# Layers 2 and 3 of a four-layer cross-attention kernel: two stages one after the other, or common slots ten tiles apart

## The chip, the cores and the metric

The kernel runs on one core of a Trainium2 chip, all in float32 but for one small mask. The metric is the device time of one launch in microseconds; the value of a kernel is the median of its runs. The core has five engines that run their own instruction lists in order and wait for one another by semaphores: PE (TensorE, matrix products and transposes by an identity, into PSUM), DVE (VectorE), ACT (ScalarE), POOL (GpSimd), and SP, which here only issues DMAs. PEld is PE's loading of weights.

## The reference

Four layers follow one another on `x` of shape (4, 1024, 256); the context has 77 rows per batch, and there are 16 heads. Layer 0 is attention over itself and the context, with a feed-forward part; layer 1 is a linear and a windowed attention. The change is in layers 2 and 3, here with projections cut to a line each:

```python
def layer2(x, ctx, mask, weights):            # mask, weights: (4, 16, 1024, 77)
    q, k, v = heads(x @ Wq.T + bq), heads(ctx @ Wk.T + bk), heads(ctx @ Wv.T + bv)
    scores = einsum('bhqd,bhkd->bhqk', q, k) / sqrt(16) * weights
    p = softmax(where(mask, -inf, scores))
    x = x + unheads(p @ v) @ Wo.T + bo
    return layernorm(x) * gamma + beta
def layer3(x, ctx):
    normed = x * rsqrt(mean(x * x) + 1e-6) * norm_w
    q, k, v = heads(normed @ wq), heads(ctx @ wk), heads(ctx @ wv)   # 64 per head
    return x + unheads(softmax(q @ k.T) @ v) @ wo
```

## The kernel before, in words

The 4096 rows are 32 tiles of 128 rows, eight to a batch; the whole of x stays in SBUF. What depends on the context alone has been folded and kept in DRAM during layer 0: `kept_k` and `kept_v` for layer 2, `kept_g` (wq times the keys, "G") and `kept_u` (the values times wo, "U") for layer 3. A tile's scores of both layers are 16 x 77 = 1232 columns.

The order of instructions is the order of the Python code (`tc.manual_schedule()`, L100); each engine takes its own in that order. After layer 1 the pool `late` is opened and the stage that concerns us runs, through L1841, as a chain of *slots*.

**Layer 2's slot, `slot2` (L1457).** In slot i work stands for tiles i, i-1, i-3, i-4 and i-5. For tile i PE makes the scores (`ps`, in a pair of PSUM banks, pool `big`, two of them), DVE multiplies them by the side weights (L1485) and masks them (`copy_predicated`, L1490), and takes the maxima of each head (`nm`, L1510 and L1514). For tile i-1 ACT makes 16 Exps of 77 columns (L1473), DVE sums and inverts (`den`, L1526 and L1527), POOL divides (L1528). For tile i-3 PE turns the ten chunks of 128 columns (`turned`, L1369: `psT` in three tiles of the PSUM pool `sm`, copied by ACT to `pT`). For tile i-4 PE multiplies by the values (`pvT`, pool `sm`), and ACT copies the result (`oT`, L1507). For tile i-5 PE multiplies by Wo (`po2`, in the one bank of pool `pv`), DVE adds to x (L1520) and POOL adds the bias (L1521). The side weights and mask of a tile, 770 KB, are loaded by SP one tile ahead (`load_sides`, L1449).

**Layer 3's slot, `slot3` (L1574).** For tile i PE makes the scores from the normed features `xT3` and G in two halves, DVE takes the maxima of each half from PSUM and subtracts them (L1599, L1600), ACT makes one Exp of 1232 columns (L1608), DVE sums and POOL divides (L1613). For tile i-2 PE turns the chunks, four before the first half of the scores, four between the halves and two after, and then multiplies by U (`po3`), DVE adds to x (L1623) and SP stores the tile.

**Between the slots** stand jobs that are doled out over a batch's eight slots: `prep2` (the next batch's queries: 16 transposes with copies on DVE, and 16 matmul instructions), `norm2` (L1532: the layernorm of a whole batch, when layer 2 is done with it: statistics on DVE, `inv_std` on POOL with a `pow`, `away` = -mean/std on POOL, then for each tile an Identity on ACT (L1543) and two products on POOL), `stats3` and `features3` (the RMS norm and `xT3` of a batch: `xn` on DVE, transposes `ptx` in `sm`, evicted on DVE with the weight), `loads2` and `loads3` (V, G and U of a batch), and the rest of layer 1 (`combine1`). Layer 3's first slots run beside the last five of layer 2, which only drain it.

PSUM is shared by all of these: `sm` has three tiles, used in turn by psT, pvT, ptx, pp2 and others, so a new one waits for the reader of the third last.

Of the kernel before, what the change touches and what calls it, by code (L numbers as in the profile page):

```python
# [17 lines left out]
P = 128  # L18
# [9 lines left out]
SC = 0.25  # L28
# [3 lines left out]
def tile_xattn_seq(ctx: ExitStack, tc: tile.TileContext, d: dict, out: bass.AP):  # L32
# [252 lines left out]
    def inv_std(rs, mv, eps, rms):  # L285

        if rms:
            nc.gpsimd.tensor_tensor(rs, mv[:, :, 0], mv[:, :, 0], ALU.mult)
            nc.gpsimd.tensor_tensor(rs, rs, mv[:, :, 1], ALU.add)
            nc.gpsimd.tensor_scalar_add(rs, rs, eps)  # L290
        else:
            nc.gpsimd.tensor_scalar_add(rs, mv[:, :, 1], eps)
        nc.gpsimd.tensor_tensor(rs, rs, nhalf, ALU.pow)
# [1084 lines left out]
    def new_scores():  # L1378
        s = late.tile([P, P * NC], F32, name="s", tag="s", bufs=4)
        nc.gpsimd.memset(s[:, HK:], 0.0)  # L1380
        return s
# [11 lines left out]
    def load_folded(b):  # L1393

        U = late.tile([P, NC, D], F32, name="U3", tag="qu")
# [6 lines left out]
        return U  # L1402

    def loads2(b):

        V = late.tile([P, NC, D], F32, name="V2", tag="qu").rearrange("p c n -> p (c n)")
        V = V[:, 0 : (NC + 1) * P].rearrange("p (c n) -> p c n", n=P)
# [18 lines left out]

    def prep2(b):

        x = xs[b]
        xT = late.tile([P, 2, T], F32, name="xT2", tag="xT")  # L1430
        yield from to_features(xT, lambda i: x[:, i, :], None, None, None, None)
        qT = late.tile([P, 2, T], F32, name="qT2", tag="gs")
        for o in range(2):
            for q in range(2):
                pp = sm.tile([P, 512], F32, name="pp2", tag="sm")
                for c in range(2):
                    mm(
                        pp, l2["Wq"][:, c, P * o : P * o + P], xT[:, c, 512 * q : 512 * q + 512],
                        start=(c == 0), stop=(c == 1),
                    )  # L1440
# [4 lines left out]
                if o and q:  # L1445
                    shared["b2", b] = qT
                yield

    def load_sides(i):  # L1449
        b, t = divmod(i, NT)  # L1450
        side = late.tile([P, HK + HK // 4], F32, name="side", tag="side")
# [5 lines left out]
    def slot2(i, tiles, at, gap2):  # L1457


        p1, p3, p4, p5 = (tiles.get(i - k) for k in (1, 3, 4, 5))  # L1460
        a = None
        if i < NB * NT:
            b, t = divmod(i, NT)
            a = tiles[i] = dict(b=b, t=t)
            qT, kb = shared["b2", b], shared["k2"]
            fs, mk = shared.pop(("side", i))
            if i + 1 < NB * NT:
                load_sides(i + 1)
            s = a["s"] = new_scores()
        if p1:  # L1470
            for h in range(H):
                hs = p1["s"][:, S * h : S * h + S]
                nc.scalar.activation(hs, hs, AF.Exp, bias=p1["nm"][:, h : h + 1], scale=SC)  # L1473
        if a:
            for o in range(2):
                ps = pair_tile()
                for e in range(2):
                    r = half_rows(e)
                    mm(
                        ps[:, e, 0 : 4 * S].rearrange("p (h s) -> p h s", s=S),  # L1480
                        qT[r, o, P * t : P * t + P],
                        kb[r, o, :, b, :],
                    )
                so = slice(o * HH * S, (o + 1) * HH * S)
                nc.vector.tensor_tensor(  # L1485
                    s[:, so].rearrange("p (i n) -> p i n", i=2), ps[:, :, 0 : 4 * S],
                    fs[:, so].rearrange("p (i n) -> p i n", i=2), ALU.mult,
                )
            sv = s[:, 0:HK]
            nc.vector.copy_predicated(sv, mk, low.to_broadcast([P, HK]))  # L1490
        gap2(at + 0.4)
        if p5:
            xt = xs[p5["b"]][:, p5["t"], :]
            po = pvp.tile([P, D], F32, name="po2", tag="pv")
            for o in range(2):
                mm(po, p5["oT"][:, o, :], l2["Wo"][:, o, :], start=(o == 0), stop=(o == 1))
            del tiles[i - 5]
        if p4:

            V = shared["v2", p4["b"]]  # L1500
            pv = sm.tile([P, 2, P], F32, name="pvT", tag="sm")
            for k in range(NC + 1):
                o, c = (0, k) if k < 5 else (1, k - 1)
                r = slice(0, rows_in(c))
                mm(pv[:, o, :], V[r, k, :], p4["pT"][r, c, :], start=k in (0, 5), stop=k in (4, NC))
            oT = p4["oT"] = late.tile([P, 2, P], F32, name="oT", tag="oT")
            nc.scalar.copy(oT, pv)  # L1507
        if a:
            nm = a["nm"] = small.tile([P, H], F32, name="nm", tag="m16")
            nc.vector.tensor_reduce(  # L1510
                nm, sv.rearrange("p (h k) -> p h k", k=S), axis=AX.X, op=ALU.max
            )

            nc.vector.tensor_scalar(nm, nm, 0.1 * NEG, -SC, ALU.max, ALU.mult)  # L1514
        if p3:
            pT = p3["pT"] = late.tile([P, NC, P], F32, name="pT", tag="pT", bufs=3)
            for g in range(3):
                turned(p3["s"], g, pT)
        if p5:
            nc.vector.tensor_tensor(xt, po, xt, ALU.add)  # L1520
            nc.gpsimd.tensor_tensor(xt, xt, rows["bo"], ALU.add)  # L1521
        gap2(at + 1.0)
        if p1:
            s3 = p1["s"][:, 0:HK].rearrange("p (h k) -> p h k", k=S)
            den = small.tile([P, H], F32, name="den", tag="den")
            nc.vector.tensor_reduce(den, s3, axis=AX.X, op=ALU.add)  # L1526
            nc.vector.reciprocal(den, den)  # L1527
            nc.gpsimd.tensor_tensor(  # L1528
                s3, s3, den.unsqueeze(2).to_broadcast([P, H, S]), ALU.mult
            )  # L1530

    def norm2(b):  # L1532

        x = xs[b]
        res = []
        yield from stats_job(res, lambda t: x[:, t, :], 1e-5, False)
        mv, rs = res
        away = small.tile([P, NT], F32, name="away", tag="away")
        nc.gpsimd.tensor_tensor(away, mv[:, :, 0], rs, ALU.mult)
        nc.gpsimd.tensor_scalar(away, away, -1.0, None, ALU.mult)  # L1540
        for t in range(NT):
            xt = x[:, t, :]
            nc.scalar.activation(  # L1543
                xt, xt, AF.Identity, bias=away[:, t : t + 1], scale=rs[:, t : t + 1]
# [3 lines left out]
            yield  # L1548


    def stats3(b):

        res = shared["st3", b] = []
        yield from stats_job(res, lambda t: xs[b][:, t, :], 1e-6, True)

    def features3(b):

        xT = shared["xT3", b] = late.tile([P, 2, T], F32, name="xT3", tag="xT")
        rs = shared["st3", b][1]
        yield from to_features(  # L1560
            xT, lambda t: xs[b][:, t, :], None, rs, cols["L3_xattn_norm_w"], None
        )

    def loads3(b):

        G = late.tile([P, 2, 8, 2, S], F32, name="G3", tag="gs")
        nc.sync.dma_start(
# [6 lines left out]
    def slot3(i, tiles, at, gap2):  # L1574
# [10 lines left out]
        for o in range(2):  # L1585
            if p2:
                turned(p2["s"], o, pT)
# [284 lines left out]
```

## Time and profile before

| | us |
|---|---|
| median of 3 runs | 2313.92 |
| lowest, highest | 2309.47, 2317.93 |
| the profiled execution's own time | 2315.16 |
| its span in the profile | 2313.4 |
| from layer 2's first scores to the end of the span (1723.3 to 2313.4) | 590.1 |

The page gives each engine's busy time, and groups instructions by line, engine, operation and tiles: count, busy time, mean duration, then the idle time of the engine just before them and who released it. In a window's row each engine's busy time is followed by its number of instructions. In a timeline row the first number is the start in us, the second the time until the end of the last of the merged instructions. A float32 matmul stands in the records as two instructions, so the ten products with U are x20. The granted clock was 0.981 over the whole span.

### The profile page before, as it was taken

The numbers are of one execution on the slowest core, as the hardware profiler recorded it, in microseconds if no ns is written. First come the engines' busy times: TensorE is split into PE (matmuls) and PEld (weight loads), VectorE is DVE, ScalarE is ACT, GpSimd is POOL, SyncE is SP. The second block draws the span as 40 slices with busy tenths as digits, with TensorE's granted clock in tenths as the row PEclk, the third lists the DMA queues.
The fourth block names the chain that finished last, engine by engine and source line by source line (L and its number), as shares of the span: only waits on it lengthen the run. The fifth ranks groups of instructions, "written<-read, shape, count | busy, mean of one in ns | idle before, by whom it ended". The sixth has DMA issues, their size and how long they took to land.

```text
span 2313.4 us, 41275 instructions
## 1 busy us (share of the span) xinstructions
PE 2167.0 (94%) x16874; PEld 1357.5 (59%) x16874; DVE 1511.2 (65%) x2492; ACT 1028.1 (44%) x1700; POOL 642.4 (28%) x927
## 2 busy tenths in 40 slices
PE   4999999999999999999989999999999998999999
PEld 2544444555555455554556675656556776788887
DVE  3756567755566555754376666777759999677664
ACT  1144444434444444344533444545548876432222
POOL 2011113111131112310152232333423655542221
PEclk9899999999999999999989999999999999999999
DMA  7221121100000000101000011101023334102200
GB/s 216 55 57 68 32 64 41 40 6 15 7 15 2 10 11 6 38 1 19 6 15 6 15 28 19 21 15 21 15 78 124 114 109 126 47 15 58 58 14 17
DMA packets 87858, 93.98 MB, mean 41 GB/s; under 512 B 35714, under 2 KB 77558, under 8 KB 87542
## 3 DMA queue, kind: packets, MB, share of 16 engines
q1 hardware_dynamic: 87670, 91.35, 15.1%
q8 instruction: 133, 2.18, 0.4%
q14 instruction: 55, 0.45, 0.1%
HBM read 55.31 MB, written 18.39 MB: 32 GB/s over the span
## 4 chain that ended last, share of the span: by engine, by line
PE 70%; DVE 14%; ACT 5%; issue 1%; POOL 1%; DVEq 0%; ACTq 0%
PE ps L51 27%; PE po L51 13%; PE pv L51 6%; PE pp L51 6%; PE ph L51 4%; DVE mpart L672 3%; PE psT L1375 2%; DVE ms L1138 2%; PE ppv L51 2%; PE pvT L51 2%; PE pvw L51 1%; DVE mrow L1142 1%; PE ptx L339 1%; PE pm L590 1%; PE pt L607 1%
## 5 line engine op out<-in xcount | busy, mean ns | idle before, releaser
L51 PE MATMUL ps<-qk 32*128 32x192 f32 (+9 forms) x6528 | 581.9, 428 | 57.8 <-DVE mpart L672 25.0
L738 ACT ACTIVATE pe<-ps 128x1024 f32<-128x1024 f32 (+2 forms) x384 | 363.3, 952 | 589.5 <-PE ps L51 581.5
L51 PEld LDWEIGHTS ps<-qk 32*128 32x128 f32 (+1 forms) x6528 | 315.9, 185 | 295.8 <-issue 75.5
L672 DVE TENSOR_REDUCE mpart<-ps 128x2 f32<-128x1024 f32 (+4 forms) x384 | 330.9, 884 | 241.9 <-PE ps L51 241.2
L741 POOL TENSOR_SCALAR_AFFINE_SELECT pe<-pe 128x256 f32<-128x256 f32 (+1 forms) x192 | 94.9, 495 | 665.5 <-ACT pe L738 664.6
L1214 ACT ACTIVATE pew<-ps 128x768 f32<-128x768 f32 x128 | 103.4, 812 | 196.4 <-PE ps L51 196.3
L1219 POOL TENSOR_SCALAR_AFFINE_SELECT pew<-pew 128x512 f32<-128x512 f32 x128 | 81.7, 638 | 338.0 <-ACT pew L1214 337.9
L1376 ACT COPY pT<-psT 128x512 f32<-128x512 f32 (+1 forms) x192 | 92.3, 518 | 175.4 <-PE psT L1375 174.9
L1138 DVE TENSOR_TENSOR ms<-ps,maskw 128x768 f32<-128x768 f32 x128 | 122.1, 954 | 69.7 <-PE ps L51 68.2
L51 PE MATMUL pv<-pe,va 128*32 128x512 f32 (+3 forms) x1536 | 157.1, 496 | 0.0
L51 PE MATMUL ph<-yT,w 128*128 128x256 f32 x512 | 143.1, 401 | 2.4 <-DVE va L401 1.0
L51 PE MATMUL po<-U,pT 128*128 128x256 f32 (+1 forms) x640 | 143.7, 379 | 0.2
L51 PE MATMUL ps<-G,xT 128*128 128x308 f32 x512 | 143.0, 423 | 0.0
L51 PEld LDWEIGHTS po<-w,hT 128*128 128x128 f32 x800 | 111.6, 192 | 47.7 <-issue 38.9
L1473 ACT ACTIVATE s<-s,nm 128x77 f32<-128x77 f32 x512 | 131.2, 347 | 17.3 <-DVE nm L1514 17.2
L51 PE MATMUL po<-w,hT 128*128 128x128 f32 (+1 forms) x800 | 138.0, 317 | 0.9 <-ACT hT L904 0.9
L665 DVE TENSOR_REDUCE mpart<-ps 128x8 f32<-128x1024 f32 x64 | 78.2, 1225 | 82.6 <-PE ps L51 82.4
L1613 POOL TENSOR_TENSOR s<-s,den 128x1232 f32<-128x1232 f32 x32 | 71.9, 2248 | 203.4 <-DVE den L1612 176.9
L51 PEld LDWEIGHTS po<-U,pT 128*128 128x128 f32 (+1 forms) x640 | 119.2, 190 | 15.5 <-ACT pT L1376 0.6
L51 PEld LDWEIGHTS ph<-yT,w 128*128 128x128 f32 x512 | 88.7, 192 | 63.9 <-issue 50.8
L1142 DVE TENSOR_REDUCE mrow<-ms 128x4 f32<-128x768 f32 x128 | 122.2, 955 | 4.4
L1375 PE MATMUL psT<-ident,s 128*128 128x128 f32 x640 | 92.9, 274 | 16.8 <-ACT oT L1507 13.0
(200 smaller groups left out, 3381.9 us busy)
## 6 DMA issues: line engine op xcount, KB each, us to landing
side<-in_fside_t SPq DMA_DIRECT2D x32, 616.0 KB
qk<-st SPq DMA_DIRECT2D x256, 64.0 KB
side<-in_mask_t SPq DMA_DIRECT2D x32, 154.0 KB
G<-kept_g SPq DMA_DIRECT2D x4, 1232.0 KB
U<-kept_u SPq DMA_DIRECT2D x4, 1152.0 KB
x<-in_x SPq DMA_DIRECT2D x8, 512.0 KB
out<-x SPq DMA_DIRECT2D x32, 128.0 KB
kept_g<-st SPq DMA_DIRECT2D x22, 154.0 KB
```

The costliest lines, as they stand in the source:

```text
L51: nc.tensor.matmul(o, lhsT, rhs, start=start, stop=stop, **kw)
L665: nc.vector.tensor_reduce(mpart[self.own][:, :, 2 * p : 2 * p + 2, 0].rearrange("p t j -> p j t"), ps.rearrange("p j (t n) -> p j t n", n= ...
L672: nc.vector.tensor_reduce(mpart[bl][:, i, 2 * p : 2 * p + 2, ci], ps[:, :, o : o + w], axis=AX.X, op=ALU.max,)
L738: nc.scalar.activation(pp[:n, :, o:512], ps[:n, :, o:512], AF.Exp, scale=SC)
L741: nc.gpsimd.affine_select(out=own, in_=own, compare_op=ALU.is_ge, fill=0.0, base=0, pattern=[[0, 2], [0, k], [1, P]], channel_multiplier=-1,)
L1138: nc.vector.tensor_tensor(v, ps.rearrange("p j (i n) -> p j i n", i=2)[:, :, :, 0:n], (maskw[:, 1:2] if w else maskw).unsqueeze(1).to_broa ...
L1142: nc.vector.tensor_reduce(mo, v, axis=AX.X, op=ALU.max, negate=True)
L1214: nc.scalar.activation(pp[:, :, :, 0 : P + WIN], ps.rearrange("p j (i n) -> p j i n", i=2)[:, :, :, 0 : P + WIN], AF.Exp, scale=SC,)
L1219: nc.gpsimd.affine_select(out=pf[:, :, 0:P], in_=pf[:, :, 0:P], compare_op=ALU.is_ge, fill=0.0, base=0, pattern=[[0, 4], [1, P]], channel_ ...
L1375: nc.tensor.transpose(ps[:, k, :], s[:, P * c : P * c + P], ident)
L1376: nc.scalar.copy(pT[:, 4 * group : 4 * group + n, :], ps[:, 0:n, :])
L1473: nc.scalar.activation(hs, hs, AF.Exp, bias=p1["nm"][:, h : h + 1], scale=SC)
```

## The change

One loop of 44 slots (`slot23`) takes the place of both chains: slot i has layer 2's tiles i (scores), i-1 (Exps, division), i-2 (transposes and values) and i-3 (Wo), and layer 3's tiles j = i-10 (scores), j-1 (division) and j-2 (transposes, product with U, store). The 16 Exps are issued in four fours. The norm after layer 2 and the RMS norm before layer 3 become one generator, `between(g)`, for four tiles at a time; it starts in slot 7+4g, and `more()`, which stands at three places of a slot, takes two steps of it, and one step of `prep2` and of `combine1`, each time. `prep2` works in two halves, and its transposes are copied by ACT. Tiles have tags of their own: s2 (3 buffers) and s3 (2), pT2 and pT3 (1 each), V2, G3 and U3 (2 each); the queries and xT3 lie in places that weights of layers 0 and 1 have left. V of the next batch and G and U of this one are loaded in slot 4 of each batch. PSUM pools are as before.

```diff
-    def new_scores():
-        s = late.tile([P, P * NC], F32, name="s", tag="s", bufs=4)
+    def new_scores(tag, bufs):
+        s = late.tile([P, P * NC], F32, name=tag, tag=tag, bufs=bufs)
...
-    def load_folded(b):
-        U = late.tile([P, NC, D], F32, name="U3", tag="qu")
+    def loads3(b):
+        G = late.tile([P, 2, 8, 2, S], F32, name="G3", tag="G3", bufs=2)
+        nc.sync.dma_start(
+            out=G.rearrange("p c f e s -> p (c f e) s"),
+            in_=kept_g.rearrange("p c f e (b s) -> p (c f e) b s", s=S)[:, :, b, :],
+        )
+        U = late.tile([P, NC, D], F32, name="U3", tag="U3", bufs=2)
...
-        return U
+        shared["b3", b] = (G.rearrange("p c f e s -> p c (f e s)"), U)
+        yield
     def loads2(b):
-        V = late.tile([P, NC, D], F32, name="V2", tag="qu").rearrange("p c n -> p (c n)")
-        V = V[:, 0 : (NC + 1) * P].rearrange("p (c n) -> p c n", n=P)
+        V = late.tile([P, NC + 1, P], F32, name="V2", tag="V2", bufs=2)
...
+    def turned_x(dst, rows, g):
+        for c in range(2):
+            pt = sm.tile([P, 4, P], F32, name="ptx", tag="sm")
+            for i in range(4):
+                nc.tensor.transpose(pt[:, i, :], rows[i][:, c * P : (c + 1) * P], ident)
+            src = pt.rearrange("p i n -> p (i n)")
+            if g is None:
+                nc.scalar.copy(dst[:, c, :], src)
+            else:
+                nc.vector.tensor_scalar(dst[:, c, :], src, g[:, c : c + 1], None, ALU.mult)
+            yield
     def prep2(b):
-        xT = late.tile([P, 2, T], F32, name="xT2", tag="xT")
-        yield from to_features(xT, lambda i: x[:, i, :], None, None, None, None)
-        qT = late.tile([P, 2, T], F32, name="qT2", tag="gs")
-        for o in range(2):
-            for q in range(2):
+        qT = wpool.tile([P, 2, T], F32, name="qT2", tag=("s2", "s4")[b % 2])
+        shared["b2", b] = qT
+        for q in range(2):
+            xT = late.tile([P, 2, 512], F32, name="xT2", tag="xT2", bufs=1)
+            yield from turned_x(xT, [x[:, 4 * q + i, :] for i in range(4)], None)
+            for o in range(2):
                 pp = sm.tile([P, 512], F32, name="pp2", tag="sm")
...
-    def slot2(i, tiles, at, gap2):
...
+    def stats4(st, mv, rs, g, eps, rms):
+        b, t0 = divmod(4 * g, NT)
+        for k in range(4):
+            nc.vector.bn_stats(st[:, k], xs[b][:, t0 + k, :])
+            nc.vector.bn_aggr(mv[:, k], st[:, k])
+            if k == 3:
+                inv_std(rs, mv, eps, rms)
+            yield
+    def between(g):
+        b, t0 = divmod(4 * g, NT)
         x = xs[b]
-        res = []
-        yield from stats_job(res, lambda t: x[:, t, :], 1e-5, False)
-        mv, rs = res
-        away = small.tile([P, NT], F32, name="away", tag="away")
+        st = small.tile([P, 4, 6], F32, name="st4", tag="st6")
+        mv = small.tile([P, 4, 2], F32, name="mv4", tag="mv", bufs=3)
+        rs = small.tile([P, 4], F32, name="rs4", tag="rs", bufs=3)
+        yield from stats4(st, mv, rs, g, 1e-5, False)
+        away = late.tile([P, 4], F32, name="away", tag="away")
         nc.gpsimd.tensor_tensor(away, mv[:, :, 0], rs, ALU.mult)
         nc.gpsimd.tensor_scalar(away, away, -1.0, None, ALU.mult)
-        for t in range(NT):
-            xt = x[:, t, :]
+        for k in range(4):
+            xt = x[:, t0 + k, :]
             nc.scalar.activation(
-                xt, xt, AF.Identity, bias=away[:, t : t + 1], scale=rs[:, t : t + 1]
+                xt, xt, AF.Identity, bias=away[:, k : k + 1], scale=rs[:, k : k + 1]
             )
             nc.gpsimd.tensor_tensor(xt, xt, rows["gamma"], ALU.mult)
             nc.gpsimd.tensor_tensor(xt, xt, rows["beta"], ALU.add)
             yield
-    def stats3(b):
...
-    def features3(b):
...
-    def slot3(i, tiles, at, gap2):
...
+        st = small.tile([P, 4, 6], F32, name="st4", tag="st6")
+        mv = small.tile([P, 4, 2], F32, name="mv4", tag="mv", bufs=3)
+        rs = small.tile([P, 4], F32, name="rs4", tag="rs", bufs=3)
+        yield from stats4(st, mv, rs, g, 1e-6, True)
+        xn = []
+        for k in range(4):
+            xt = small.tile([P, D], F32, name="xn", tag="xn", bufs=4)
+            normed(xt, x[:, t0 + k, :], None, rs, k)
+            xn.append(xt)
+            if k % 2:
+                yield
+        xT = shared["xT3"][:, g % 2]
+        yield from turned_x(xT, xn, cols["L3_xattn_norm_w"])
+    LAG = 10
...
+    def score2(a, i):
+        b, t = a["b"], a["t"]
+        qT, kb = shared["b2", b], shared["k2"]
+        fs, mk = shared.pop(("side", i))
+        if i + 1 < NB * NT:
+            load_sides(i + 1)
+        s = a["s"] = new_scores("s2", 3)
...
+    def exps2(a, heads):
+        for h in heads:
+            hs = a["s"][:, S * h : S * h + S]
+            nc.scalar.activation(hs, hs, AF.Exp, bias=a["nm"][:, h : h + 1], scale=SC)
+    def divided(a, tag):
+        s3 = a["s"][:, 0:HK].rearrange("p (h k) -> p h k", k=S)
+        den = late.tile([P, H], F32, name=tag, tag=tag)
+        nc.vector.tensor_reduce(den, s3, axis=AX.X, op=ALU.add)
+        nc.vector.reciprocal(den, den)
+        nc.gpsimd.tensor_tensor(
+            s3, s3, den.unsqueeze(2).to_broadcast([P, H, S]), ALU.mult
+        )
+    def turned_all(a, tag):
+        pT = a["pT"] = late.tile([P, NC, P], F32, name=tag, tag=tag, bufs=1)
+        for g in range(3):
+            turned(a["s"], g, pT)
...
+    def out2(a):
+        xt = xs[a["b"]][:, a["t"], :]
+        po = pvp.tile([P, D], F32, name="po2", tag="pv")
+        for o in range(2):
+            mm(po, a["oT"][:, o, :], l2["Wo"][:, o, :], start=(o == 0), stop=(o == 1))
+        nc.vector.tensor_tensor(xt, po, xt, ALU.add)
+        nc.gpsimd.tensor_tensor(xt, xt, rows["bo"], ALU.add)
...
+    def slot23(i, two, three, more):
+        n = NB * NT
+        j = i - LAG
+        a2, p2, q2, r2 = (two.get(i - k) for k in range(4))
+        a3, p3, q3 = (three.get(j - k) for k in range(3))
+        if i < n:
+            a2 = two[i] = dict(zip("bt", divmod(i, NT)))
+        if 0 <= j < n:
+            a3 = three[j] = dict(zip("bt", divmod(j, NT)))
+        if q3:
+            turned_all(q3, "pT3")
         if p2:
+            exps2(p2, range(4))
+        if a2:
+            score2(a2, i)
+        more()
         if p2:
+            exps2(p2, range(4, 8))
+        if p3:
+            divided(p3, "den3")
+        if q3:
+            out3(q3)
         if p2:
+            exps2(p2, range(8, 12))
+        if a2:
+            maxima2(a2)
+        if a3:
+            score3(a3, j)
+        if p2:
+            exps2(p2, range(12, H))
+        more()
+        if q2:
+            turned_all(q2, "pT2")
+        if r2:
+            out2(r2)
+        if a3:
+            nc.scalar.activation(a3["s"][:, 0:HK], a3["s"][:, 0:HK], AF.Exp)
+        if p2:
+            divided(p2, "den2")
+        more()
+        if q2:
+            values_of2(q2)
+        two.pop(i - 3, None)
+        three.pop(j - 2, None)
...
-    run(slots(slot3, 2, jobs3, slots(slot2, 5, jobs2)))
+    two, three, live2 = {}, {}, []
+    def xT3_place():
+        shared["xT3"] = wpool.tile([P, 2, 2, 512], F32, name="xT3", tag="s1")
+        yield
+    def more():
+        for e in list(live2):
+            gen, each = e[:2]
+            for _ in range(each):
+                if next(gen, StopIteration) is StopIteration:
+                    live2.remove(e)
+                    break
+    for i in range(NB * NT + LAG + 2):
+        b, k = divmod(i, NT)
+        if i == 0:
+            live2.append((combine1(NB - 1, 1), 1))
+        if i == 6:
+            run(xT3_place())
+        if k == 4:
+            if b + 1 < NB:
+                run(loads2(b + 1))
+            if b < NB:
+                run(loads3(b))
+        if k == 1 and b + 1 < NB:
+            live2.append((prep2(b + 1), 1))
+        if i >= 7 and (i - 7) % 4 == 0 and (i - 7) // 4 < NB * NT // 4:
+            live2.append((between((i - 7) // 4), 2))
+        slot23(i, two, three, more)
+    assert not live2 and not two and not three
```

## The prediction

> **What bounds the kernel now.** I read the page first, then the windows view with one window for layer 2's slots (from its first score product) and one for layer 3's.
>
> ```profile
> span 2313.4 us, 41275 instructions
> PE 2167.0 (94%) x16874; PEld 1357.5 (59%) x16874; DVE 1511.2 (65%) x2492; ACT 1028.1 (44%) x1700; POOL 642.4 (28%) x927
> 1723.30:1982.30 259.00, 228.72 (x1467) 178.36 (x1467) 240.78 (x343) 200.57 (x670) 134.72 (x155) 0.95 0.34 110
> 1982.30:2313.40 331.10, 325.83 (x1624) 267.19 (x1622) 210.88 (x330) 97.03 (x148) 101.56 (x103) 1.00 0.13 36
> ```
>
> After the window's length come PE, PEld, DVE, ACT and POOL busy, the granted clock, and DMA. Layer 2 is held by DVE (240.8 of 259.0 us, PE idle for 30), layer 3 by PE (325.8 of 331.1). The change can touch these 590.1 us and no others. PE's 554.6 us is the floor if all overlapped; so at most 36 us, 1.5%, is to be had (a little more, as layer 2's clock stood at 0.95). The waits and the group list of layer 2 come next.
>
> ```profile
> ACT x L1543 <- POOL away L1540: 12.8, 3, 6.4
> PE psT L1375 <- ACT oT L1507: 11.5, 5, 4.2
> PE psT L1375 <- DVE xT L343: 1.9, 2, 1.5
> L1528 POOL TENSOR_TENSOR s<-s,den 128x1232 f32<-128x1232 f32 x31 | 69.7, 2249 | 72.0 <-DVE den L1527 66.9 <-PE ps L51 5.1
> ```
>
> Three times, once for each batch normed in layer 2, ACT stood before the norm's Identity for POOL's `away`, up to 6.4 us. Behind it on ACT stood the oT copy, which frees one of the three `sm` banks, and PE's transposes stood for that bank (11.5 us). The timeline of one such place, and of a slot of layer 3:
>
> ```profile
> 1892.14 0.25 POOL L1540 TENSOR_SCALAR away<-away 128x8 f32<-128x8 f32 x1
> 1892.43 0.60 ACT L1543 ACTIVATE x<-x,away,rs 128x256 f32<-128x256 f32 x1 [3.24 <-POOL away L1540]
> 1898.31 0.69 PE L1375 MATMUL psT<-ident,s 128*128 128x128 f32 x2 [4.23 <-ACT oT L1507]
> ...
> 2106.60 2.24 PE L51 MATMUL ps<-G,xT 128*128 128x308 f32 x8
> 2108.88 0.80 DVE L1599 TENSOR_REDUCE m<-ps 128x8 f32<-128x616 f32 x1 [0.37 <-PE ps L51]
> 2108.90 4.49 PE L51 MATMUL po<-U,pT 128*128 128x256 f32 x20
> 2109.72 0.80 DVE L1600 TENSOR_TENSOR s<-ps,m 128x616 f32<-128x616 f32 x1
> 2110.61 1.23 ACT L1608 ACTIVATE s<-s 128x1232 f32<-128x1232 f32 x1 [1.14 <-DVE s L1600]
> ```
>
> In layer 3, PE multiplies by U (4.5 us) right after the scores, so DVE's 0.8 + 0.8 and ACT's 1.23 run under it. Last, the clock after two idle gaps, in windows of 2 us:
>
> ```profile
> 1920.00:1922.00 2.00, 0.64 (x6) 0.15 (x2) 1.93 (x5) 0.14 (x1) 0.00 (x0) 1.00 0.45 160
> 1922.00:1924.00 2.00, 1.51 (x9) 1.41 (x10) 1.93 (x7) 1.80 (x8) 0.73 (x1) 1.00 0.66 232
> 1928.00:1930.00 2.00, 0.40 (x4) 0.00 (x0) 1.93 (x5) 0.00 (x0) 1.02 (x4) 1.00 0.44 59
> 1930.00:1932.00 2.00, 1.45 (x4) 1.20 (x5) 1.18 (x3) 1.73 (x7) 1.98 (x2) 0.75 0.93 336
> 1932.00:1934.00 2.00, 2.00 (x11) 1.96 (x10) 1.97 (x5) 2.00 (x9) 0.00 (x0) 0.50 1.17 278
> 1934.00:1936.00 2.00, 2.00 (x18) 2.00 (x18) 1.96 (x4) 0.50 (x3) 1.83 (x1) 0.90 1.26 242
> ```
>
> The third number from the end is the granted clock. A gap of 1.84 us (before 1922.5) kept it full; one of 2.15 us (before 1930.6) was followed by 1.0 + 2.0 + 0.4 = 3.4 us at half, which costs 1.7 us of dense PE work.
>
> **The change, part by part.** PE's parts of a tile, from the timeline and the chain: ten transposes 1.1 us, layer 2's scores 1.2, its values 2.5, its Wo 0.9; layer 3's scores 4.2, its U product 4.3. A common slot is 1.1+1.2+4.3+4.2+1.1+0.9+2.5 = 15.3 us of PE. DVE's: layer 2, 1.5 (two products) + 1.6 (mask) + 1.45 and 0.2 (maxima) + 1.7 (den) + 0.4 = 6.85; layer 3, 3.2 + 1.7 + 0.4 = 5.3; the norm of four tiles 4.7 (eight stats) + 1.7 (xn) + 1.5 (xT) = 7.9, so 2.0 per tile: 14.1. PE is the longer, narrowly. There are 44 slots, of which 20 (12 to 31) are full; 0 to 9 hold layer 2 alone, 34 to 43 layer 3 alone.
>
> Slots 0 to 9: DVE as before, 4.9 for the first, 7 for each of the next two (with combine1's adds), 7.05 with handovers for each of seven, plus the norm's share (2.4 in slot 7, 2.4 in 8, 3.2 in 9): 76.3. The Identity's wait (below) adds about 5: **81**.
>
> Slots 10 to 31 without waits: 10 and 11 lack the U product but hold prep2 and the first stats, 13 + 14; twenty at 15.3 = 306; norm transposes 5 x 0.9; one prep2 (16 transposes, 16 products) 8.7: 346.2. Now the waits, from the engines' order in `slot23`:
>
> (a) *The norm's first slot.* `more` stands at three places, two steps of `between` at each. Counting from a slot's start T, DVE: first score half at T+1.9, products and mask +3.1, two stats +1.2, den3 +1.7, add +0.4, maxima +1.4 and +0.7 (the nm row took 1.39 instead of 0.17 beside a POOL division), four readings of layer 3's scores +3.2, handovers +0.3: T+13.9. Then two stats to 15.1, out2's add, den2 to 17.2. POOL in order: inv_std 2.1 (15.1 to 17.2), the bo add 0.7, den2's division 2.25, away 0.55: T+20.75. Two Identities of 0.6 stand on ACT ahead of oT: oT is out at T+22.3. PE has ended the slot's work at 15.3, does eight of the next ten transposes, and stands at 16.2 for the bank: 6.1 us, and some 1.9 us for the half clock after it. Six groups begin in slots 11 to 31 (11, 15, ... 31): 6 x 8.0 = 48. This is the wait of before, eight times instead of four. Its bounds are 0 (were DVE 6 us ahead) and 10 each; I take the row's mechanism with the full queue, since DVE's list is nearly as long as PE's.
>
> (b) *The norm's third slot.* Here turned_x puts two `sm` tiles ahead of layer 2's transposes, and DVE frees them only after layer 3's readings: 13.9 - 1.2 + 1.7 (xn) + 0.75 = T+15.15, while PE comes there at 12.15. The waits on DVE xT in before are at most 1.5 us; by this count 3.0, with 0.5 for the clock: 5 x 3.5 = 17.5, bounds 0 and 5 each.
>
> Together slots 10 to 31 take **411.7**. Slots 32 and 33 (both layers still, no new scores of layer 2) are 2 x 14.1 plus one (b) and 0.9 for its transposes: **32.6**.
>
> (c) *Layer 3 alone.* In `slot23` the ten transposes stand first and the U product right behind, where slot3 had them among the scores. On ACT the Exp of the tile just scored is ahead of the pT copies. After the last score: 0.8 + 0.8 + 1.23 + 0.59 (copy) + 0.4 of handovers = 3.85 us until U can start, less 1.1 for transposes: PE stands 2.75 us in every slot. What covered this before (the U product itself) is gone. Slot 34 takes 10.5; seven slots 67.2 + 0.9; gaps 1.9 + 6 x 2.75 = 18.4; the last group's Identity 4.5; slots 42 and 43, whose U products wait for their copies and division, 13.9; add and output 3.2 as now. The clock: 2.75 us is above the 2.15 that halved it, but not far; I let 6 in 10 of the eight gaps halve it, 8 x 0.6 x 1.7 = 8 (bounds 0 and 14). Sum **126.6**.
>
> The Trainium skill ("TensorE: Matmul & The Clock Gate", section "Why this matters for your kernels") warns only of idle gaps over about 3 us; the trace's 2.15 us gap differs, and the trace decides. By the page's figure (c) and (b) would be about 10 us cheaper.
>
> *At nothing:* prep2's copies move from DVE (8.1 us) to ACT, idle by 58 us of 259; the chain ahead of the first scores grows by two handovers and copies, 1.5 us. loads2 and loads3 now queue V, G and U (3.2 MB) on SP ahead of a side load; G and U kept the DMAs busy for 15 us in before (1929 to 1944), and the side tile behind them is needed some 20 us after they are issued. If that cover is short, 3 to 10 us once. The halved groups double inv_std and away on POOL (about 10 us more, POOL 236 busy of 590); they count only in (a).
>
> Sum: 81 + 411.7 + 32.6 + 126.6 + 1.5 = 653.4, against 590.1: +63 us. The profiled run took 2315.2 (span 2313.4 and 1.8 around it), 1.3 above the median, 2313.9; 63 on the median makes 2377.
>
> **The rivals.** *(1) Faster: the waits of the norm vanish.* If DVE runs ahead of PE in the common slots, Identity's release comes before PE needs the bank. Then 76.3 + 346.2 + 29.1 + 122.1 (c without the Identity's 4.5) + 1.5 = 575, 15 us less: 2299. For it: 15.3 of PE against 14.1 of DVE. Against it: POOL's four pieces (5.6 us) come after den2 or its stats, the last thing DVE does in a slot. It decides from (a) under about 3 us a group; own range 2280 to 2320.
> *(2) Half the waits*, where DVE drifts ahead in the slots without stats: (a) 4, (b) 1.5 a group: 2377 - 24 - 10 - 8 = 2335; range 2320 to 2352.
> *(3) DVE becomes the bound*, as POOL's longer day holds it at nm and xn (rows of 0.17 grew to 1.39): 2 us more in 20 slots: 2415.
> *(4) The slots don't overlap as the words say*, since only 20 of 44 are full: that is in the sum, not apart from it.
>
> **How the numbers follow.** Forecast 0.58 (own range 2352 to 2403), rival 1 0.15, rival 2 0.22, rival 3 0.05. No change means within 0.3%, 7 us, about what a measurement can tell: from rival 1's upper part 0.04, from rival 2's lower edge 0.03. Faster 0.11, same 0.07, slower 0.82. The range runs from 2308 to 2405, leaving the 0.11 below and less than 0.1 above.
>
> **What would show it.** Right: in slots 10 to 33 PE idles in lumps of 4 to 6 us every fourth slot, before psT, released by ACT oT, with ACT's Identity waiting for POOL `away` about eight times, 30 us or more in all; every fourth slot psT waits for DVE's ptx eviction; after the last scores of layer 2 PE waits 2 to 3 us before each po3, released by ACT pT, and the clock falls under 0.95 there, where it was 1.00. Wrong: PE solid in common slots of 15 to 16 us (rival 1), or DVE solid at 17 or more (rival 3); a wait for `side` near slot 5 would put the SP queue on the list.

## The result, and the profile after

The changed kernel takes **2383.94 us** (median of 4 runs, 2380.47 to 2387.88) against 2315.4 for the kernel before (median of 4 runs, its first three among them): a ratio of 1.03, 95% interval 1.027 to 1.033. It is slower, by 68.5 us. The profiled execution took 2380.6 us with a span of 2378.9. The page's first lines:

```profile
span 2378.9 us, 41163 instructions
PE 2174.4 (91%) x16842; PEld 1369.1 (58%) x16874; DVE 1492.3 (63%) x2476; ACT 1027.1 (43%) x1716; POOL 649.9 (27%) x959
```

The engines' work is what it was (PE 7 us more, DVE 19 less), so all that was lost is waiting and clock. The windows view, cut at layer 2's scores of tile 0, of tile 10, at the end of slot 31 and of slot 33 (columns as before: length, PE, PEld, DVE, ACT, POOL, granted clock, DMA):

```profile
1720.16:1831.86 111.70, 81.75 (x466) 62.31 (x465) 72.97 (x101) 60.36 (x195) 34.67 (x41) 0.88 0.32 100
1831.86:2218.77 386.91, 360.09 (x2014) 291.43 (x2014) 293.06 (x443) 195.64 (x555) 159.53 (x192) 0.97 0.24 71
2218.77:2254.98 36.21, 31.06 (x175) 26.25 (x174) 19.33 (x35) 14.34 (x36) 19.50 (x24) 0.95 0.02 8
2254.98:2378.90 123.92, 99.54 (x442) 79.56 (x440) 50.35 (x83) 24.85 (x43) 30.58 (x34) 0.92 0.03 11
```

From the first scores to the end that is 658.7 us; before it was 590.1. The prediction had 81, 411.7, 32.6 and 126.6. The sum came out within 7 us, but by two errors against each other: the first line is 31 us too short in the prediction, the second and third together 21 too long. In the first line neither PE (82 of 112 us) nor DVE (73) is full.

The waits (in the columns the engine, its tile and line, who released it; total, times, longest):

```profile
ACT x L1497 <- POOL away L1494: 35.8, 8, 6.9
PE psT L1375 <- ACT oT L1580: 25.4, 6, 5.0
PE po L51 <- ACT pT L1376: 19.0, 7, 5.3
DVE s L1537 <- DMA side<-in_fside_t: 11.0, 2, 9.4
PE psT L1375 <- POOL s L1562: 10.7, 4, 5.9
```

The first three are those that the prediction named in (a) and (c); the fourth is the wait for `side` that it named as a sign that the SP queue, there "at nothing", belongs on the list. Step (a) in the timeline, slot 11 (the start, the time to the end of the last merged instruction, engine, line):

```profile
1857.59 0.18 DVE L1479 BATCH_NORM_AGGREGATE mv<-st 128x2 f32<-128x6 f32 x1
1858.18 1.04 POOL L293 TENSOR_TENSOR rs<-rs,nhalf 128x4 f32<-128x4 f32 x1
1859.19 0.72 POOL L1588 TENSOR_TENSOR x<-x,r_bo 128x256 f32<-128x256 f32 x1
1859.87 2.25 POOL L1562 TENSOR_TENSOR s<-s,den 128x1232 f32<-128x1232 f32 x1
1862.36 0.24 POOL L1494 TENSOR_SCALAR away<-away 128x4 f32<-128x4 f32 x1
1862.64 1.09 ACT L1497 ACTIVATE x<-x,away,rs 128x256 f32<-128x256 f32 x2 [4.67 <-POOL away L1494]
1863.63 0.35 ACT L1580 COPY oT<-pvT 128x256 f32<-128x256 f32 x1
1864.04 0.69 PE L1375 MATMUL psT<-ident,s 128*128 128x128 f32 x2 [5.02 <-ACT oT L1580]
1864.65 2.42 PE L51 MATMUL ps<-kb,qT 64*128 64x308 f32 x8
```

POOL reaches `away` only after `pow`, bo and the division; ACT holds the oT copy behind the two Identities; PE stands 5.02 us for the bank; and the scores behind take 2.42 us at half clock instead of 1.31. Step (c), slot 36, with layer 3 alone:

```profile
2296.55 1.23 ACT L1661 ACTIVATE s<-s 128x1232 f32<-128x1232 f32 x1 [11.13 <-DVE s L1609]
2297.69 1.33 ACT L1376 COPY pT<-psT 128x512 f32<-128x512 f32 x3
2298.31 6.27 PE L51 MATMUL po<-U,pT 128*128 128x256 f32 x20 [2.37 <-ACT pT L1376]
```

The Exp of the tile just scored is ahead of the pT copies; PE stands 2.37 us, and the product with U takes 6.27 us instead of 4.59.

### The profile page after: what moved, and what is told of

It is laid out like the page before. It is cut to its first block, busy times and chain, and to the rows that moved or that the text cites. A ratio compares the mean times of both kernels' runs of the same rounds, so it can differ in the third digit from the quotient of the medians.

```text
span 2378.9 us, 41163 instructions
## 1 busy us (share of the span) xinstructions
PE 2174.4 (91%) x16842; PEld 1369.1 (58%) x16874; DVE 1492.3 (63%) x2476; ACT 1027.1 (43%) x1716; POOL 649.9 (27%) x959
## 4 chain that ended last, share of the span: by engine, by line
PE 66%; DVE 15%; ACT 5%; POOL 2%; issue 2%; DMA 1%; SPq 0%; DVEq 0%; ACTq 0%; POOLq 0%
PE ps L51 25%; PE po L51 13%; PE pv L51 6%; PE pp L51 5%; PE ph L51 4%; DVE mpart L672 3%; PE pvT L51 2%; DVE ms L1138 2%; PE psT L1375 2%; PE ppv L51 2%; PE pvw L51 1%; DVE mrow L1142 1%; PE pt L607 1%; PE pm L590 1%; ACT pe L738 1%
## 5 line engine op out<-in xcount | busy, mean ns | idle before, releaser
L1562 POOL TENSOR_TENSOR s<-s,den 128x1232 f32<-128x1232 f32 x64 | 143.9, 2248 | 192.7 <-DVE den L1561 185.0
L51 PE MATMUL po<-U,pT 128*128 128x256 f32 (+1 forms) x640 | 159.6, 408 | 19.3 <-ACT pT L1376 19.0
L51 PEld LDWEIGHTS po<-U,pT 128*128 128x128 f32 (+1 forms) x640 | 128.6, 205 | 50.3 <-ACT pT L1376 27.5
L1376 ACT COPY pT<-psT 128x512 f32<-128x512 f32 (+1 forms) x192 | 87.1, 519 | 135.1 <-PE psT L1375 133.0
L51 PE MATMUL ps<-G,xT 128*128 128x308 f32 x512 | 137.9, 422 | 0.0
```

The costliest lines, as they stand in the source:

```text
L51: nc.tensor.matmul(o, lhsT, rhs, start=start, stop=stop, **kw)
L1376: nc.scalar.copy(pT[:, 4 * group : 4 * group + n, :], ps[:, 0:n, :])
L1562: nc.gpsimd.tensor_tensor(s3, s3, den.unsqueeze(2).to_broadcast([P, H, S]), ALU.mult)
```

## The experiments

The theory was the prediction's own: the norm's order on POOL and ACT (a), layer 3's order in the slots that it has alone (c), and, after the result, the SP queue in slots 5 and 6. The table collects what was measured. The stage runs from the first scores of layer 2 to the end of the span in the profiled execution; its parts are cut at the scores of tile 10 and of tile 31. The first scores themselves began anywhere from 1720 to 1727 us in these profiles, also where the kernels are the same up to there; this is in the times and not in the stages. Gains are against the changed kernel unless another is named.

| kernel | median us | ratio to before, 95% | stage | tiles 0-9 | 10-30 | from 31 |
|---|---|---|---|---|---|---|
| after | 2383.94 | 1.027 to 1.033 | 658.7 | 111.7 | 372.7 | 174.3 |
| 1 Identity later | 2345.36 | 1.0113 to 1.0151 | 618.7 | 108.6 | 343.2 | 167.0 |
| 2 order alone | 2358.81 | 1.0173 to 1.0216 | 630.1 | 111.8 | 372.9 | 145.4 |
| 3 loads split | 2373.43 | 1.0235 to 1.0288 | 648.2 | 101.5 | 372.7 | 174.0 |
| 4 copies on DVE | 2392.26 | 1.0318 to 1.0357 | 665.2 | 112.0 | 378.8 | 174.4 |
| 5 away first | 2377.58 | 1.0257 to 1.0298 | 649.7 | 112.4 | 362.7 | 174.6 |
| 6 prep2 spread | 2384.39 | 1.0275 to 1.0326 | 655.4 | 106.2 | 374.7 | 174.4 |
| 7 apart | 2485.25 | 1.0722 to 1.0778 | 757.6 | | | |
| 8 = 1 + 2 + 3 | 2306.73 | 0.9944 to 0.9972 | 578.6 | 98.6 | 339.8 | 140.2 |
| 9 = 8, values later | **2299.01** | 0.9904 to 0.9942 | 571.9 | 89.4 | 342.2 | 140.3 |
| 10 = 8, prep2 shifted | 2315.80 | 0.9987 to 1.0009 | 588.1 | 108.2 | 339.7 | 140.2 |
| 11 = 9 + 10 | 2311.67 | 0.9971 to 0.9997 | 582.3 | 99.9 | 342.2 | 140.2 |

**1. The Identity two steps later.**

```diff
         yield from stats4(st, mv, rs, g, 1e-5, False)
+        yield
+        yield
         away = late.tile([P, 4], F32, name="away", tag="away")
```

> Two blank steps stand between the statistics of between and its Identities, so that away has four or five us more to be ready and ACT meets the Identities in the next slot, behind the pT copies. The theory (what the change lost in the common slots are waits in order: ACT before the Identity for POOL, oT behind it, PE's transposes behind oT): PE's waits on ACT oT, 25.4 us in 6 gaps, nearly vanish, with the half clock after them some 1.5 us each; with the places in slots 7 and 35, 30 to 42 us less, about 2348. The rival (PE and DVE are both nearly full in the common slots, so that the next wait takes the place of the one removed, here DVE's xn for POOL's second statistics or psT for DVE's ptx copies): under 12 us less, 2372 or more.

Measured: 38.6 us off by the medians, 40.0 by the stage. PE's waits for oT are gone from the list. The windows of tiles 10 to 30, first of after, then of this kernel:

```profile
1831.86:2204.61 372.75, 345.93 (x1935) 279.60 (x1934) 280.11 (x421) 188.28 (x534) 155.46 (x187) 0.97 0.25 74
```

```profile
1833.54:2176.69 343.15, 337.67 (x1934) 275.49 (x1933) 284.70 (x421) 189.21 (x534) 154.63 (x184) 1.00 0.26 80
```

With the same instructions PE's idle time falls from 27 to 5 us and its busy time by another 8, for the clock is whole. Five groups begin here and give 29.5 us, so (a) is worth about 5.9 us a group. The window from tile 31, in which the groups of slots 31 and 35 begin, gives 7.3 more, and tiles 0 to 9, with the group of slot 7, 3.1. Common slots without the norm's transposes or prep2 then come every 15.4 us, one after another (timeline of this kernel):

```profile
2048.85 1.31 PE L51 MATMUL ps<-kb,qT 64*128 64x308 f32 x8
2064.26 1.31 PE L51 MATMUL ps<-kb,qT 64*128 64x308 f32 x8
```

**2. Layer 3 alone in `slot3`'s order.** In slots 34 to 41 the chunks' transposes stand among the score halves again, and the product with U behind the scores. Three score tiles are then alive at once, so the edit also moves them from s3's two buffers to s2's three; in the changed kernel nothing waited for a buffer of s3.

```diff
+        if a3 and q3 and not a2 and not q2:
+            divided(p3, "den3")
...
+            score3(a3, j, "s2", 3, lambda o: turned(q3["s"], o, pT))
+            turned(q3["s"], 2, pT)
...
+            nc.scalar.activation(a3["s"][:, 0:HK], a3["s"][:, 0:HK], AF.Exp)
+            out3(q3)
```

> In the slots 34 to 41, where layer 3 is alone, the transposes stand among the scores again, as in the kernel before, and the U product behind them. The theory (ACT's Exp of the tile just scored stands before the pT copies and holds the U product): PE's waits on ACT pT, 19.0 us in 7 gaps, and the half clock after some of them go; the stretch from slot 34 to the end (123.9 us) shrinks to about 98, so 20 to 28 us less, about 2360. The rival (another wait is behind it: POOL's division, or DVE): under 8 us less.

Measured: 25.1 us off, 28.9 of the stage from tile 31 on, and nothing elsewhere. That window, of after and of this kernel:

```profile
2204.61:2378.90 174.29, 144.76 (x693) 117.64 (x692) 82.63 (x138) 46.54 (x102) 54.14 (x63) 0.94 0.03 10
```

```profile
2209.75:2355.20 145.45, 135.97 (x693) 111.58 (x692) 81.83 (x138) 48.67 (x102) 54.21 (x63) 0.99 0.04 12
```

PE's idle time goes from 29.5 to 9.5 us, its busy time down by 8.8 with the clock. Of the idle time that is left, 4.3 us are the gap of (a) in this window.

**3. The loads split.** What the trace of after shows on SP ahead of slot 5 (the queue's own timeline; lines left out are loads of the same kind):

```profile
1737.49 0.43 SPq L1417 DMA_DIRECT2D V<-kept_v  x1
1759.80 0.33 SPq L1420 DMA_DIRECT2D V<-kept_v  x1
...
1761.56 0.62 SPq L1396 DMA_DIRECT2D G<-kept_g  x1
1762.23 4.62 SPq L1403 DMA_DIRECT2D U<-kept_u  x1
...
1768.44 0.37 SPq L1470 DMA_DIRECT2D side<-in_fside_t  x1
```

SP stood 22 us between the first and the second line, for POOL's memset of V, which POOL reaches only in slot 4 (it ran from 1759.46 to 1759.77; the waits name the memset that follows it on POOL). Then V, G and U went out ahead of the next side weights. These were issued at 1768.44, 1.6 us after the scores that they belong to had begun, and landed 7.7 us later; DVE waited 9.4 us for them:

```profile
SPq L1420 <- POOL s L1380: 21.9, 1, 21.9
```

```profile
1776.21 1.50 DVE L1537 TENSOR_TENSOR s<-ps,side 128x616 f32<-128x616 f32 x2 [9.40 <-DMA side<-in_fside_t]
```

The experiment issues V's memset, V, G and U in slots 2, 3, 4 and 6:

```diff
-        if k == 4:
-            if b + 1 < NB:
-                run(loads2(b + 1))
-            if b < NB:
-                run(loads3(b))
+        if k == 2 and b + 1 < NB:
+            loading = loads2(b + 1)
+            next(loading)
+        if k == 3 and b + 1 < NB:
+            run(loading)
...
```

> V's memset is put in slot 2 of each batch, V's DMAs in slot 3, G's in slot 4 and U's in slot 6. The theory (in slots 4 and 5 SP's queue first stood for POOL's memset of V and then issued V, G and U ahead of the side weights, and DVE waited for these 11.0 us in two places, then everybody for the clock and for POOL's division): the wait for side goes, slots 0 to 9 take 10 to 16 us less, about 2371. The rival (the prediction's, that the loads cost nothing because other waits are there anyway): within 5 us of 2384.

Measured: 10.5 us off; the wait for `side` is gone, and slots 5 and 6 take 7.7 us each instead of 10.3 and 15.2. The edit removes the wait for the memset and the crowd of loads ahead of `side` at once; what each alone would cost no run shows.

**4. prep2's copies back on DVE.**

```diff
-                nc.scalar.copy(dst[:, c, :], src)
+                nc.vector.tensor_copy(dst[:, c, :], src)
```

> The copies of prep2's transposes go back from ACT to DVE. The theory (in slots 1 to 3 the copies stand behind up to 12 Exps on ACT and hold the sm banks, 4.3 us of PE's waits by the rows, and the Exps stand behind the copies): slots 1 to 3, 34.5 us, shrink by 5 to 9, while the common slots lose nothing, about 2377. The rival (DVE is the fuller engine in the common slots, 293 of 387 us against ACT's 196, so its 0.7 us a copy return there): 0 to 6 us more than 2384.

Measured: 8.3 us slower; 6.1 of it lie in tiles 10 to 30, where slot 17, with prep2, took 22.8 us instead of 20.3, and next to nothing (0.3) in tiles 0 to 9. The change's move of these copies to ACT is a gain, and the theory that it lengthened slots 1 to 3 fell.

**5. `away` ahead of the division.** The third `more()` stands before `divided(p2, "den2")`.

> Only the order on POOL (and of den2 on DVE) at a slot's end is changed: the third call of more stands before den2 and its division, so away goes ahead of a division of 2.25 us; the Identities keep their place on ACT ahead of oT. The theory (the Identity waits for POOL's queue, piece by piece): PE's gaps before psT released by oT shrink by 2.2 us each, from 4.3 to about 2, below the gap that halves the clock: six times 2.2 + 1.5, so 15 to 25 us less, about 2364. The rival (the Identity waits for DVE's late statistics or den2, and POOL's order doesn't matter): 0 to 5 us less.

Measured: 6.4 us off, 9.0 of the stage, between the rival's 0 to 5 and the theory's 15 to 25. The same place as in after, for the group of slot 27 (timeline):

```profile
2148.97 0.24 POOL L1494 TENSOR_SCALAR away<-away 128x4 f32<-128x4 f32 x1
2149.25 1.09 ACT L1497 ACTIVATE x<-x,away,rs 128x256 f32<-128x256 f32 x2 [2.42 <-POOL away L1494]
2150.66 0.44 PE L1375 MATMUL psT<-ident,s 128*128 128x128 f32 x2 [2.14 <-ACT oT L1580]
```

The division's 2.25 us left the chain and the gap fell by as much, from 4.34 to 2.14 us; but `pow`, the bo add and the Identities are still in it, and the 2.14 us still halved the clock in this slot. Taking one link out shortened the wait by that link and no more. In slot 21 a wait of 3.4 us for DVE's `ptx` copy, where after had 1.2, took part of the gain back (23.0 us instead of 18.7).

**6. prep2 one step in a slot.** It starts one slot earlier and takes one step a slot instead of three.

> prep2 is taken one step a slot, at the third more, from the batch's first slot on, instead of three steps a slot in slots 1 to 3; its copies stay on ACT. The theory (crowding: combine1 and prep2 together put 5 us of PE work and their ACT copies into each of slots 1 to 3, where a slot of layer 2 alone is a chain of PE, DVE and ACT that has no room for them): slots 0 to 3 take 6 to 10 us less, slots 8 to 10 some 4 to 8 less, about 2371. The rival (the work must be done in these slots anyway, and each step now costs its own handover in eight slots): within 4 us of 2384.

Measured: no difference in the medians, 3.3 us less in the stage. Tiles 0 to 9 gained 5.5 us, but the common slots that now hold a step take 17.1 us instead of 15.4: PE is full there, so the work costs its own length wherever it lies.

**7. The layers apart.** The lag is 34 slots instead of 10, so that no slot is common, with the norms and loads moved along.

> LAG is 34 instead of 10, so that layer 3 begins when layer 2 is drained: the same slots, but never two layers side by side (between and the loads of G and U move with layer 3). The theory (a common slot of 15.4 us does the work of a slot of layer 2 alone, 7.5 us and more with prep2, and one of layer 3 alone, 12.3 to 13.7 us with its gap for pT): 32 slots of layer 2 in about 285 us, 2 drains 14, 34 slots of layer 3 in 440, together some 740 against 659: about 2465. The rival (PE's work is the bound whatever stands beside what): 2384 within 15.

Measured: 2485, 20 us over the theory and far from the rival's 2384. Windows of layer 2's slots and of layer 3's:

```profile
1719.85:2025.76 305.91, 241.80 (x1558) 188.19 (x1557) 222.19 (x281) 198.44 (x672) 106.57 (x113) 0.96 0.32 101
2025.76:2477.40 451.64, 361.21 (x1534) 285.19 (x1532) 214.67 (x379) 93.95 (x157) 138.21 (x176) 0.91 0.07 21
```

Before, these were 259.0 and 331.1 us. So the overlap itself is worth about 100 us; it has to make up for two slot bodies that are each slower than `slot2` and `slot3`. Layer 3 loses 3.8 us a tile, for the most part by (c): PE stood 77 us for ACT's pT copies, 17 times for 2.4 us and 7 times, where Identities of the norm stood ahead as well, for 4.1 to 5.4, and its busy time is 35 us longer at a granted clock of 0.91.

```profile
PE po L51 <- ACT pT L1376: 77.1, 24, 5.4
```

Layer 2 loses 47 us too, with most norms not even in it, and this the prediction did not have; experiment 9 takes it up.

**8. The three repairs together.** Edits 1, 2 and 3.

> e1, e2 and e3 together: blank steps before the Identities, layer 3's own order in slots 34 to 41, split loads. The theory (three separate waits): 38.6 + 25.1 + 10.5 less, but for 4 us of the last group's Identity in slot 35, which both e1 and e2 took: 70 us less, about 2314, the time of the kernel before. The rival (the waits cover one another): 2330 or more.

Measured: 2306.73 us, 77.2 off where the three alone give 38.6 + 25.1 + 10.5 = 74.2. This is 0.3 to 0.6% under the kernel before. The three did not cover one another; in tiles 10 to 30 they helped: with edit 1 alone DVE waited 2.3 us for `side` in slot 13, which took 20.9 us, and with edit 3 as well it takes 17.7.

**9. The values one slot later.** What is left in tiles 0 to 9 is a chain. In kernel 8 a slot with layer 2 alone takes 7.67 us; DVE's list is 6.8. The timeline of kernel 8:

```profile
1773.44 0.25 DVE L1566 RECIPROCAL den<-den 128x16 f32<-128x16 f32 x1
1773.83 2.25 POOL L1567 TENSOR_TENSOR s<-s,den 128x1232 f32<-128x1232 f32 x1 [0.97 <-PE pvT L51]
1776.14 1.31 PE L1375 MATMUL psT<-ident,s 128*128 128x128 f32 x10 [1.14 <-POOL s L1567]
1778.71 2.72 PE L51 MATMUL pvT<-pT,V 128*128 128x128 f32 x22 [0.40 <-ACT pT L1376]
1781.36 1.31 PE L51 MATMUL ps<-kb,qT 64*128 64x308 f32 x8
1782.26 1.51 DVE L1542 TENSOR_TENSOR s<-ps,side 128x616 f32<-128x616 f32 x2 [0.88 <-PE ps L51]
```

From the end of the reciprocal through division, transposes, copies and values to the start of the next tile's scores it is 7.67 us, and DVE stands for these scores. `slot2` had the transposes two slots after the division and the values a slot later; its DVE products followed at 6.64 us (trace of before):

```profile
1767.03 1.44 DVE L1485 TENSOR_TENSOR s<-ps,side 128x616 f32<-128x616 f32 x2
1773.67 1.44 DVE L1485 TENSOR_TENSOR s<-ps,side 128x616 f32<-128x616 f32 x2
```

The edit puts the values behind the next tile's scores while layer 2 is alone:

```diff
             score2(a2, i)
+        if r2 and i <= LAG:
+            values_of2(r2)
         more()
...
-        if q2:
+        if q2 and i >= LAG:
             values_of2(q2)
```

> Base: the kernel with the three edits together (2306.7 us). In slots 0 to 9 the product with the values is made one slot later, behind the next tile's scores, so that the chain division 2.25, ten transposes, pT copies, 22 products 2.7 no longer stands ahead of the scores on PE. Theory: layer 2 alone runs at 7.67 us a slot because this chain and DVE's 6.8 us follow one another (two slots 15.34); without it a slot goes to DVE's own 6.8 to 6.9, and slots 2, 3 and 8, where the transposes came late, get 1 to 3 us shorter: 5 to 10 us in all, 2297 to 2302. Rival: DVE's own list and its hand-overs set 7.67, and nothing moves: 2305 to 2309.

Measured: **2299.01**, 7.7 less than kernel 8, as the theory had it. The same DVE line in kernel 9, now without a wait:

```profile
1771.36 1.45 DVE L1542 TENSOR_TENSOR s<-ps,side 128x616 f32<-128x616 f32 x2
1778.08 1.45 DVE L1542 TENSOR_TENSOR s<-ps,side 128x616 f32<-128x616 f32 x2
```

That is 6.72 us. Slots 4 to 7 take 27.3 instead of 30.7, slot 2 10.7 instead of 13.2, slot 8 10.3 instead of 14.9; slots 9 and 10 give 3.6 back, where the order changes over. This is the fastest of all, 0.6 to 1.0% under the kernel before.

**10 and 11. The first prep2 in slots 4 to 6.** Begun at `k == 4` instead of `k == 1` for batch 0, on kernel 8 and on kernel 9.

> Base: the kernel with the three edits together (2306.7 us), in which slots 2 and 3 take 13.2 and 13.4 us and slots 4 to 7 take 7.7 each. The first prep2 is begun in slot 4 instead of slot 1, so that it no longer meets combine1. Theory: its ACT copies stand behind the Exps and PE's queue behind the copies, wherever it lies: slots 1 to 3 get some 9 us shorter, slots 4 to 6 as much longer, the whole within 3 us of 2306.7. Rival: what costs is the meeting of prep2 and combine1 in the same slots; apart, both fit into what PE has free (1.5 us a slot) and the time falls by 5 to 8 us, to 2299 to 2302.

> Both edits together on the kernel with three edits (2306.7 us): values one slot later in slots 0 to 9, and the first prep2 from slot 4. If the chain through the values is what prep2's late copies act on, prep2 costs less here than by its shift alone: 8 to 14 us off, 2293 to 2299. If not, no better than the better one of the two edits.

Measured: 2315.80 and 2311.67, both worse than without the shift. Theory and rival of the tenth missed; of the eleventh the gain missed, and its "if not" came. Slots 1 to 3 gained only 4.6 us (12.9 and 12.1 for slots 2 and 3, without prep2 in them), slots 4 to 6 lost 12.6. The length of slots 2 and 3 is thus not mainly prep2: with it in them PE stood before a transpose for its `xT` copy (2.8 us in kernel 8), without it for the first tile's division (3.9 us in kernel 10). What of it belongs to combine1 and what to the pipeline's filling no run tells apart.

## Why the prediction was right, and where its terms were not

The time fell in the forecast's own range, and the mechanisms (a) and (c) are shown by experiments 1 and 2: taking each away returned 38.6 and 25.1 us, nearly all where it stood. Step by step:

- **Common slots**, 15.3 us: measured 15.4, PE solid. Right; rival 3 (DVE at 17 or more) is out. The overlap of the slots is worth about 100 us (experiment 7).
- **(a)**, 8.0 us a group: 5.9 by experiment 1. The mechanism and the chain were right. The six gaps were 5.02, 4.34, 3.08, 4.33, 4.34 and 4.34 us, not 6.1. They were read too high in two places: `pow` over four columns takes 1.04 us where the row of before, over eight, has 1.67, which with its handovers shortened the chain by 1.0, and in the gaps of 4.3 us DVE's statistics ended 1.9 us before PE stopped, not 1.1. Five gaps were followed by a half clock; half of the time that PE worked under it is 1.5 to 3.0 us each, 1.9 a group over all six, as in the sum. Rival 1 needed under 3 us a group and is out. Rival 2's 4 was about as far off as the forecast's 8.0.
- **(b)**, 3.5 us a group: some 1.0 us of wait, most of it for ACT's copy that frees the one bank left over (3.2 us in all) and less for DVE's of `ptx` (1.7), and with the split transposes about 1.3 (a slot with ptx takes 17.6 against 15.4, of which the prediction had 0.9 as work). Mis-sized, and rival 2's 1.5 was the better size: in slot 13 DVE had the first half evicted 13.9 us after the slot's start, not 15.15; half of this is that the four `xn` took 1.1 us and not 1.7.
- **(c)**, 2.75 us a slot: 2.37 to 2.43 in five of the eight, 1.56 in slot 34, next to none in slot 37, where the norm's transposes and a wait of 1.1 us behind them cover it, and 5.35 in slot 35 with the last group's Identities: 19.0 us in all, against 18.4 and 4.5 for these Identities. Right. The clock fell after four of its six gaps over 2 us and cost 7.2 us in all, against 8 in the sum.
- **Slots 0 to 9**, 81 us: 111.7. This is the step that failed, in three terms. The loads on SP, "at nothing", cost 10.5 us (experiment 3): the 20 us of cover were counted from the moment of issue, but SP issued late, as it stood 22 us for a POOL instruction. DVE's 7.05 us a slot took DVE for the bound; a chain over two slots was (experiment 9), worth another 7 to 9 us. And 7 us each for slots 1 and 2 and 7.05 for slot 3 left out what holds PE while the pipeline fills; these three took 8.0, 13.1 and 13.4 us. Of that, 2.5 went with the chain in experiment 9; the rest is open.
- **prep2's copies on ACT**, at nothing: right, and more (experiment 4). Its chain ahead of the first scores grew from 9.7 to 10.5 us, against 1.5 in the sum.

So the forecast was right in its sign and in its two causes; that it was right to 7 us is luck: (a) and (b), some 20 us too dear, stood against slots 0 to 9, 31 us too cheap. With these slots as predicted the time would have been about 2353, where the forecast's own range and rival 2's meet. That the change lost, although its overlap works, lay in its placement: three waits, each cured by an edit of a few lines, turn 68 us of loss into 9 of gain, and the fourth makes it 17.

On the clock, the prediction held the trace's 2.15 us gap against the Trainium skill ("TensorE: Matmul & The Clock Gate", section "Why this matters for your kernels"), which warns of gaps over about 3 us. The runs again show half clocks after shorter gaps: in layer 3's slots 2.37 us halved it, of four gaps of 2.43 us two did, and a gap of 3.08 us in a common slot did not. The length of the gap alone decides neither way.

The clock records of the thirteen traces show what does. Every change of the granted clock lies on a grid of equal stretches of 3.41 us, and what counts is PE's idle time (no product and no transpose) inside one stretch. From 1700 us on there are 2283 stretches at full clock: all 120 with more than 1.97 us of idle time were followed by a stretch at half clock, none of the 2125 with less than 1.73 us was, and of the 38 between them 11 were. The gaps of 2.43 us put 1.78, 2.05, 1.97 and 2.43 us into one stretch, and the second and the fourth halved the clock; the gap of 3.08 us fell into two stretches, 1.77 and 1.31.

## What to carry to other kernels

When two stages are merged into common slots, write down for each engine what stands ahead of the one copy that frees a shared PSUM bank: a small chain (`pow`, `away`, Identity) that stood in PE's way three times in layer 2 of the kernel before stops it once every group here. Keep the old order for the slots that only one stage uses, and the old distance between its steps: a pipeline two slots shorter made a chain the bound where an engine had been. And count a load's cover from the moment when its queue can issue it, with the waits of everything queued before it, not from its place in the code.

## What the runs showed of the hardware

- POOL's `pow` costs 1.04 us for 128x4 and 1.67 for 128x8, so two halved groups pay 2.08 us where one whole group pays 1.67.
- Gaps of the same length differ in what the clock does after them: 2.43 us in four successive slots of layer 3 was followed by 4.59, 6.06, 4.59 and 6.27 us for the same product with U. In these traces the clock halved where PE had been idle for more than 1.97 us inside one stretch of its 3.41 us grid.
- One wait in the SP queue, on a memset that POOL came to 22 us later, held back every load issued behind it on that queue: `side` left 1.6 us after its scores had begun.
